# Four graph layers on 64 graphs: every issue time of a written-out plan replaced

## The chip, the cores and the metric

The kernel runs on one core of a Trainium2 chip, in one launch. The metric is the device time of that launch in microseconds (us). Several runs of the kernel before are given with their median; one more execution was profiled.

## The reference, cut to what matters

There are 64 independent graphs of 256 nodes with 512 features each, and a 256 x 256 adjacency matrix per graph. Each graph passes through four layers. Every layer begins with a layer norm over the features and a ReLU, and adds its result to `x`. All data are float32.

```python
# layer 0
h = relu(layernorm(x)); q, k = split(h @ W_qk); v = h @ W_v
x = x + softmax(sum((q @ k.T) / 8 * adj, -1), over nodes) * v
# layer 1: 8 heads of 64
h = relu(layernorm(x)); f = h @ W[head]
att = softmax(leaky_relu(e_self[:, None] + e_neigh[None, :]) + NEG_BIG * (1 - adj))
x = x + relu(att @ f + b)
# layer 2: 8 heads
h = relu(layernorm(x)); Xp = h @ Wp + bp; Xc = Xp @ C.T
x = x + relu(tanh(adj * (Xc @ Xp.T)) @ Xp)
# layer 3
h = relu(layernorm(x)); q, k = split(h @ W_qk); v = h @ W_v
x = x + softmax(q . (adj @ (k * mask)) / sqrt(512), over nodes) * v
```

## The kernel before, in words

**Steps and the plan.** The work of one graph is cut into 178 named steps. A step issues one to eight instructions on one engine, or DMAs on the queue of SyncE (SP). A table gives each step an issue time: `TIMES` holds the times for a graph in the steady state, relative to the start of its period; `FIRST` has tables of their own for the first nine graphs, `LAST` for the last eight, and `WEIGHTS` for the loading and preparing of the weights. A step of graph `b` gets the time `b * PERIOD + TIMES[step]`. `Plan.sequence` (line 619) sorts all steps of all graphs by that time, and `Plan.run` (line 627) issues them in this order and ties each instruction to the one before it on the same engine, so that no compiler moves them:

```python
steps += [(b * PERIOD + at, b, name) for name, at in times.items()]
return sorted(steps)
```

The times are not waited for on the chip. They only fix the order in which the instructions stand in each engine's queue. On the chip an engine takes its queue in order, and each instruction waits on semaphores for its own inputs and buffers. So five or six graphs are under way at once, interleaved step by step. Buffers (`big`, `bank`, `xt` and so on) are taken from lists when a step is issued and put back when their last user has been issued.

**The steps that matter here.** A name ends in the layer or in a part number.

- Layer 0: `load` (six DMAs), `st0 rs0 pw0 sh0 hn0` (norm), `sq0` (two 32 x 32 block transposes on VectorE, line 912), `sw0` (one DMA that writes the 512 KB tile to DRAM, line 1029), `ht0` (four DMAs that gather it transposed, line 917). Then `vsa`, `vsb` on GpSimd (lines 1065 to 1073) make sums, from which seven products `v1` to `v7` on TensorE (line 1081, two-by-two block products in seven multiplications) give `v` and the scores; `v1`, `v2`, `v4` need only what `ht0` brought, `v5`, `v6`, `v7`, `v3` need `vsa` or `vsb` too. VectorE adds them up (`vu vq vl0 vw vl1 vr0 vr1`, line 1095), `score0` (TensorE, line 1197), `s0v`, `softp0` (TensorE, line 1037), `softv0 softa0 softw0`, `add0`.
- Layer 1: `ms1 sx1 rs1 pw1 sh1 hn1 sq1 sw1 ht1` as above; `fa0`, `fa1` (TensorE, line 906, 272 columns wide), `fae0`, `fae1`, `send` (VectorE, lines 1246 to 1265), `er` (four small DMAs to DRAM), `enes` (two DMAs of 1 MB that bring the rows back to all partitions, lines 1275 and 1276); `max0` to `max3` (VectorE, line 1288, sixteen instructions), `mxv mxt mr mb`; per pair of heads `ea` (ScalarE), `eg` (GpSimd, line 1334), `eb` (VectorE, line 1340), `ex` (ScalarE), `po` (TensorE, line 1358), `eh` (GpSimd, line 1367); `sqo0`, `sqo1`, `swo` and `or` send the result through DRAM (lines 1163, 1029, 1179).
- Layer 2: `xp0 xp1` (line 906, 512 wide), `xe`, `sqx swx xpt`, `xc`, `ps0 ps1`, `tv`, `ta`, `py0 py1`, `sqy0 sqy1 swy yr`.
- Layer 3: `agg0 agg1` (line 1550), `sq3 sw3 ht3`, seven products `g1` to `g7` as in layer 0, `zs`, `softp3`, `add3`, `store`.

Every sheet that has to be transposed thus goes to DRAM and back (`sw` then `ht`), seven times for a graph, all on SP's queue.

Of the kernel before, what the change touches and what calls it, by code (L numbers as in the profile page):

```python
# [37 lines left out]
PERIOD = 53.0  # L38
TIMES = {
    "load": -55.958, "st0": -49.583, "rs0": -44.646, "pw0": -36.318, "sh0": -34.389, "hn0": -28.054, "sq0": -23.880,  # L40
    "sw0": -20.361, "at": -13.629, "ht0": -13.295, "vsa": -7.391, "vsb": -5.585, "v5": -5.238, "v6": -4.473,
    "v1": -4.435, "v2": -4.429, "va": -3.714, "v7": -3.586, "vu": -3.459, "v4": -0.672, "v3": -0.428, "vq": 0.560,
    "vw": 0.888, "vl0": 1.080, "vl1": 1.174, "score0": 1.287, "s0v": 2.823, "vr0": 3.678, "softp0": 6.233,
    "softv0": 7.190, "softa0": 8.025, "vr1": 8.143, "softw0": 11.863, "add0": 11.883, "ms1": 12.017, "sx1": 12.176,
    "rs1": 12.570, "pw1": 15.448, "sh1": 15.468, "hn1": 17.606, "sq1": 17.626, "sw1": 20.639, "ht1": 21.979,
    "fa0": 22.725, "fa1": 23.304, "fae0": 26.098, "fae1": 27.361, "send": 27.471, "er": 31.505, "enes": 34.142,
    "neg": 38.100, "max0": 40.266, "max2": 40.311, "ea1": 46.119, "max3": 47.873, "max1": 47.890, "negt": 49.291,
    "ea2": 51.375, "ea3": 55.720, "eg1": 57.348, "ea0": 61.604, "mxv": 61.732, "mxt": 61.752, "fb0": 64.897,
    "fbe0": 64.917, "mr": 70.776, "mb": 70.796, "eg3": 75.379, "eg2": 75.479, "fb1": 75.603, "eg0": 75.679,
    "fbe1": 77.982, "eb0": 78.082, "ex0": 78.102, "eb3": 78.275, "eb1": 78.325, "ex1": 78.337, "eb2": 78.397,  # L50
    "eh1": 79.204, "ex3": 79.228, "po0": 80.231, "po1": 80.682, "ex2": 80.783, "po2": 84.620, "po3": 85.301,
    "sqo0": 85.445, "eh0": 88.783, "su0": 88.910, "sqo1": 91.326, "eh3": 91.549, "swo": 91.587, "eh2": 94.253,
    "su1": 94.458, "se": 94.478, "or": 94.836, "sp": 95.038, "sr": 98.701, "om0": 101.429, "om1": 101.861,
    "oa0": 101.861, "oa1": 101.881, "sx2": 102.438, "rs2": 103.930, "pw2": 103.950, "sh2": 104.354, "hn2": 104.374,
    "sq2": 107.686, "sw2": 109.636, "ht2": 119.000, "xp0": 125.880, "xe0": 126.367, "xp1": 127.317, "xe1": 128.965,
    "sqx": 129.657, "swx": 130.649, "xpt": 135.864, "xc": 138.845, "xcv": 146.041, "xca": 146.061, "ps1": 146.081,
    "tv2": 146.101, "tv3": 146.151, "ta2": 149.074, "ps0": 149.878, "tv1": 150.250, "ta3": 150.686, "py1": 151.759,
    "tv0": 151.889, "ta1": 152.589, "ta0": 152.972, "py0": 154.569, "sqy0": 155.545, "sqy1": 158.087, "swy": 160.787,
    "yr": 168.125, "yp0": 169.206, "yp1": 169.226, "ya1": 171.370, "ya0": 171.420, "sx3": 174.829, "rs3": 174.849,
    "am": 177.436, "pw3": 178.663, "sh3": 179.490, "hn3": 179.510, "sq3": 179.709, "sw3": 180.291, "agg1": 181.480,  # L60
    "agg0": 181.703, "ht3": 186.025, "gsa": 195.020, "ga0": 195.034, "g4": 196.820, "ga1": 197.203, "zd": 198.118,
    "gsb": 200.495, "g2": 200.888, "g5": 202.877, "g6": 213.565, "g1": 219.162, "xa": 221.007, "g3": 224.216,
    "uu": 224.644, "g7": 225.065, "uq": 227.417, "uw": 227.437, "zc": 227.478, "uc1": 230.511, "za": 233.117,
    "zb": 234.865, "zs": 235.303, "softp3": 235.361, "softv3": 242.009, "uc0": 243.772, "softa3": 248.324,
    "softw3": 248.344, "add3": 248.611, "store": 256.387,
# [3 lines left out]
    "wn0": -2754.166, "mt0": -2695.235, "mv0": -2547.881, "mm0": -2545.730, "wa": -1191.640, "wqk": -1154.337,  # L69
    "wn1": -1149.788, "wv0": -1139.027, "mt1": -1138.916, "mv1": -1138.119, "t0": -1137.526, "w10": -1127.290,  # L70
    "sa0": -1126.945, "b1": -1092.446, "wn2": -988.967, "mm1": -985.862, "wn3": -953.396, "w11": -932.270,
    "sa1": -887.977, "mt2": -885.804, "w12": -880.346, "w13": -874.980, "mv2": -504.503, "mt3": -499.542,
    "mm2": -499.507, "sa3": -487.647, "sa2": -487.190, "mv3": -407.047, "w21": -337.874, "wv3": -333.465,
    "mm3": -316.473, "mk": -300.627, "mkp": -208.048, "ma": -204.797, "w22": -179.666, "mkv": -174.873,
    "w20": -173.107, "w23": -159.368, "b2": -147.136, "c2": -38.328, "mt": -12.051, "room": 111.231,
# [1534 lines left out]
```

## Time and profile before

| what | value |
|---|---|
| runs of the kernel | 3685.83 us median of 3 (3681.97 to 3687.0) |
| the profiled execution, its own time | 3695.39 us |
| its span, first to last instruction | 3693.3 us |
| TensorE granted clock | 0.985 of full speed |
| TensorE, VectorE, ScalarE, GpSimd busy | 3494.9, 3251.5, 2415.6, 1623.2 us |
| DMA moved | 785.00 MB, mean 213 GB/s |
| store of graph 9 issued, of graph 52 issued | 783.9 us, 3145.8 us: 43 rounds of 54.93 us |

What lies around the span is 2.1 us. Between the ninth and the fifty-third graph the kernel is in a steady round of 54.93 us, one graph coming out of each; the rest is the filling at the start and the draining at the end. A busy TensorE counts pipelined matrix products from their start to a modelled end, so that its share says little of how much room is left; the distances of their starts say more.

### The profile page before, as it was taken

What the parts mean: (1) busy time and instruction counts of PE and PEld (TensorE: products, weight loads), DVE (VectorE), ACT (ScalarE), POOL (GpSimd) and SP (SyncE); (2) the same over time, 40 slices, a digit from 0 to 9 for tenths busy, and PEclk for the clock granted to TensorE, in tenths of its full rate; (3) what the DMA queues carried; (4) which work ended last, traced back from release to release, by engine and by line L of the source; (5) the groups of instructions that cost most, each with busy time, mean ns of one, the idle gap of its engine ahead of it and who ended that gap; (6) DMA issues with size and microseconds to landing.
All of it is one profiled execution on the core that took longest, in us unless ns stands there. A gap on an engine that the chain in (4) does not pass through costs nothing.

```text
span 3693.3 us, 57357 instructions
## 1 busy us (share of the span) xinstructions
PE 3494.9 (95%) x16322; PEld 2031.4 (55%) x16322; DVE 3251.5 (88%) x8558; ACT 2415.6 (65%) x5381; POOL 1623.2 (44%) x1811
## 2 busy tenths in 40 slices
PE   6889999999999999999999999999999999998988
PEld 3555555555555555555555555555555555555544
DVE  6789898999898999999999899899899999898866
ACT  2567666667667667667766767667666766656654
POOL 2454444454444454444454444354444444343441
PEclk8899999999999999999999999999999999999999
DMA  6667666776776777777777777777677777676643
GB/s 192 196 217 218 211 213 199 223 222 217 222 220 211 224 223 221 227 228 217 222 229 211 223 224 212 219 234 214 216 231 219 221 224 221 198 215 190 210 149 120
DMA packets 967467, 785.00 MB, mean 213 GB/s; under 512 B 788912, under 2 KB 859120, under 8 KB 942576
## 3 DMA queue, kind: packets, MB, share of 16 engines
q1 hardware_dynamic: 967152, 781.34, 69.0%
q8 instruction: 132, 2.16, 0.2%
q14 instruction: 183, 1.50, 0.1%
HBM read 511.12 MB, written 270.01 MB: 211 GB/s over the span
## 4 chain that ended last, share of the span: by engine, by line
DVE 32%; PE 24%; DMA 19%; ACT 10%; issue 7%; SPq 6%; POOL 2%; DVEq 0%; ACTq 0%; POOLq 0%
DMA big<-sq_d 9%; DMA sq_d<-big 9%; PE bank L1081 8%; PE bank L906 7%; DVE big L912 6%; DVE big L1095 5%; ACT big L1416 5%; DVE big L1340 4%; PE bank L1358 3%; SPq L917 2%; SPq L1179 2%; DVE big L1163 2%; ACT big L974 2%; DVE bank L1135 2%; PE bank L1487 2%
## 5 line engine op out<-in xcount | busy, mean ns | idle before, releaser
L906 PE MATMUL bank<-w_s,big 128*128 128x256 f32 (+2 forms) x3072 | 956.1, 462 | 48.7 <-DMA big<-sq_d 42.6
L906 PEld LDWEIGHTS bank<-w_s,big 128*128 128x128 f32 x3072 | 604.3, 199 | 435.1 <-issue 281.9
L1081 PE MATMUL bank<-t_s,big 128*128 128x320 f32 (+1 forms) x1536 | 610.1, 528 | 39.2 <-POOL big L1065 31.2
L996 POOL TENSOR_TENSOR rstd<-rstd,power 128x2 f32<-128x2 f32 x256 | 178.9, 699 | 1053.6 <-DVE rstd L990 999.2
L1334 POOL TENSOR_TENSOR big<-big,negt 128x1024 f32<-128x1024 f32 x256 | 605.8, 2389 | 21.6 <-ACT big L1327 18.0
L1288 DVE CUSTOM_DVE_ANT_0 junk<-all,adj 128x256 f32<-128x256 f32 x1024 | 485.9, 475 | 32.2 <-DMA all<-er_d 1.5
L1346 ACT ACTIVATE big<-big 128x1024 f32<-128x1024 f32 x256 | 258.8, 1051 | 389.6 <-DVE big L1340 388.6
L1367 POOL TENSOR_TENSOR half<-big 128x512 f32<-128x512 f32 x256 | 325.2, 1291 | 424.9 <-ACT big L1346 288.9
L1009 ACT ACTIVATE big<-xt,shift,rstd 128x512 f32<-128x512 f32 x512 | 383.4, 805 | 171.4 <-POOL shift L1002 169.2
L912 DVE STREAM_TRANSPOSE big<-big 128x512 f32<-128x512 f32 x640 | 472.6, 774 | 19.4 <-ACT big L1009 18.9
L1327 ACT ACTIVATE big<-all,ec 128x256 f32<-128x256 f32 x1024 | 428.1, 494 | 80.2 <-DMA all<-er_d 76.4
L1095 DVE TENSOR_TENSOR big<-bank,big 128x320 f32<-128x320 f32 (+1 forms) x704 | 393.9, 568 | 35.4 <-PE bank L1081 19.9
L1081 PEld LDWEIGHTS bank<-t_s,big 128*128 128x128 f32 x1536 | 280.6, 194 | 241.9 <-issue 121.3
L1511 DVE TENSOR_TENSOR big<-bank,at 128x512 f32<-128x512 f32 x512 | 318.1, 673 | 48.1 <-PE bank L1487 46.7
L1518 ACT ACTIVATE big<-big 128x512 f32<-128x512 f32 x512 | 294.1, 625 | 85.5 <-DVE big L1511 81.2
L1081 PE MATMUL bank<-w_s,big 128*128 128x320 f32 x1024 | 323.0, 448 | 11.6 <-ACT big L1103 3.8
L1065 POOL TENSOR_TENSOR big<-big 128x256 f32<-128x256 f32 x128 | 110.3, 862 | 502.9 <-DMA big<-sq_d 462.3
L1340 DVE TENSOR_TENSOR big<-big,all 128x1024 f32<-128x1024 f32 x256 | 304.0, 1245 | 1.9 <-DMA all<-m_d 1.5
L974 ACT ACTIVATE big<-xt,sum 128x512 f32<-128x512 f32 x384 | 272.7, 711 | 42.0 <-DVE sum L1226 29.1
L1416 ACT ACTIVATE big<-big,rs 128x64 f32<-128x64 f32 x1024 | 251.5, 333 | 64.0 <-DMA big<-sq_d 51.8
L1487 PE MATMUL bank<-big,big 64*128 64x256 f32 x2048 | 260.0, 392 | 4.8 <-DVE bank L1135 4.3
L1358 PE MATMUL bank<-big,big 128*64 128x256 f32 x2048 | 243.1, 386 | 17.2 <-ACT big L1346 16.7
(119 smaller groups left out, 5300.0 us busy)
## 6 DMA issues: line engine op xcount, KB each, us to landing
sq_d<-big SPq DMA_DIRECT2D x448, 512.0 KB
big<-sq_d SPq DMA_DIRECT2D x1792, 128.0 KB
all<-er_d SPq DMA_DIRECT2D x128, 1024.0 KB
all<-m_d SPq DMA_DIRECT2D x64, 1024.0 KB
xt<-in_x_dram SPq DMA_DIRECT2D x64, 512.0 KB
out_dram<-xt SPq DMA_DIRECT2D x64, 512.0 KB
adj<-in_adj_dram SPq DMA_DIRECT2D x64, 256.0 KB
blocks<-in_adj_dram SPq DMA_DIRECT2D x256, 64.0 KB
```

The source lines that it names most:

```text
L906: nc.tensor.matmul(p, chunk(ht[:, k], c), w[:, k], start=(k == 0), stop=(k == KC - 1))
L912: nc.vector.transpose(sq.rearrange("p (r k i c) -> p c k r i", r=4, k=KC, c=NC)[:, c], t[:, c])
L974: nc.scalar.activation(g["hn"][:, c, :], g["xt"][:, c, :], AF.Square, scale=-float(D), bias=st["sum"][:, c:c + 1], accum_out=st["ssq"][:, ...
L1009: nc.scalar.activation(g["hn"][:, c, :], g["xt"][:, c, :], AF.Relu, bias=st["shift"][:, c:c + 1], scale=st["rstd"][:, c:c + 1])
L1081: nc.tensor.matmul(p, a()[:, k], w[:, k], start=(k == 0), stop=(k == 1))
L1095: nc.vector.tensor_tensor(out(), g[i][:, :w], old(), OP.add)
L1288: nc.vector.tensor_tensor_reduce(junk, g["en"][:, h, :], g["adj"][:, c, :], 1.0, -BIG, OP.add, OP.max, g["mx"][:, c, h:h + 1])
L1327: nc.scalar.activation(e[:, s, j, :], g["es"][:, h, :], AF.Prelu, bias=st["ec"][:, j, H + h:H + h + 1], alpha=0.2)
L1334: nc.gpsimd.tensor_tensor(e, e, g["negt"][:, None].to_broadcast([P, 2, NC, N]), OP.add)
L1340: nc.vector.tensor_tensor(e, e, g["m"][:, 2 * p:2 * p + 2, None, :].to_broadcast([P, 2, NC, N]), OP.subtract)
L1358: nc.tensor.matmul(po[s * U:(s + 1) * U, p % 2, :], feats[:, j, h * U:(h + 1) * U], e[:, s, j, :], start=(j == 0), stop=(j == NC - 1))
L1416: nc.scalar.activation(normal_rows(2)[:, c, h * U:(h + 1) * U].rearrange("p (a i) -> p a i", a=2), y[:, h // 2, h % 2 * 2:h % 2 * 2 + 2], ...
```

## The change

Only the tables `PERIOD`, `TIMES`, `WEIGHTS`, `FIRST` and `LAST` change. No step, no instruction, no tile and no buffer count is altered; the order of the queues is. `FIRST` and `LAST` keep their nine and eight tables, with every time new. The lines of the diff that hold the steps named here:

```diff
-PERIOD = 53.0
+PERIOD = 52.8
 TIMES = {
-    "load": -55.958, "st0": -49.583, "rs0": -44.646, "pw0": -36.318, "sh0": -34.389, "hn0": -28.054, "sq0": -23.880,
-    "sw0": -20.361, "at": -13.629, "ht0": -13.295, "vsa": -7.391, "vsb": -5.585, "v5": -5.238, "v6": -4.473,
-    "v1": -4.435, "v2": -4.429, "va": -3.714, "v7": -3.586, "vu": -3.459, "v4": -0.672, "v3": -0.428, "vq": 0.560,
-    "vw": 0.888, "vl0": 1.080, "vl1": 1.174, "score0": 1.287, "s0v": 2.823, "vr0": 3.678, "softp0": 6.233,
-    "fa0": 22.725, "fa1": 23.304, "fae0": 26.098, "fae1": 27.361, "send": 27.471, "er": 31.505, "enes": 34.142,
+    "load": -39.563, "st0": -11.544, "rs0": -7.386, "pw0": -7.277, "sh0": -7.257, "neg": -6.117, "hn0": -2.912,
+    "sq0": -0.951, "sw0": 1.023, "ht0": 8.345, "vsa": 9.031, "v2": 10.708, "at": 11.189, "v1": 12.329, "v5": 12.373,
+    "va": 12.902, "v6": 13.291, "vsb": 13.821, "vu": 14.671, "vl0": 14.721, "v7": 15.867, "v4": 15.981, "vq": 18.814,
+    "vw": 19.471, "vl1": 20.118, "score0": 20.138, "s0v": 20.835, "softp0": 21.256, "v3": 22.258, "softv0": 25.597,
+    "ht1": 46.450, "fa0": 48.029, "fa1": 49.125, "fae0": 50.298, "fae1": 50.987, "send": 51.284, "er": 52.645,
+    "enes": 54.413, "max0": 61.658, "max2": 64.992, "max1": 65.589, "ea2": 66.135, "fb1": 70.598, "max3": 73.438,
...
 WEIGHTS = {
-    "wn0": -2754.166, "mt0": -2695.235, "mv0": -2547.881, "mm0": -2545.730, "wa": -1191.640, "wqk": -1154.337,
+    "wn0": -3088.720, "mt0": -3061.312, "wa": -2989.984, "mv0": -2986.374, "wn1": -2972.348, "w10": -2970.224,
...
```

Sorted, the steady tables give these queues for one round. The number in brackets is the graph relative to the one whose `score0` begins the list.

```
TensorE before: score0[0] g6[-4] softp0[0] g1[-4] fb0[-1] g3[-4] g7[-4] xp0[-2] xp1[-2] agg1[-3] fb1[-1] agg0[-3]
  fa0[0] fa1[0] softp3[-4] po0 po1 po2 po3[-1] xc[-2] su0[-1] g4[-3] ps1[-2] su1[-1] g2[-3] sp[-1] g5[-3] ps0[-2]
  py1[-2] v5[1] v6[1] v1[1] py0[-2] v2[1] v7[1] v4[1] v3[1] | score0[1] g6[-3] softp0[1] ...
TensorE after:  score0[0] g4[-4] softp0[0] v3[0] fb0[-1] g5[-4] g2[-4] xp0[-2] xp1[-2] agg0[-3] g7[-4] po2[-1]
  fa0[0] fa1[0] agg1[-3] g1[-3] softp3[-4] xc[-2] su0 po0 po1 po3 su1[-1] ps0[-2] ps1[-2] g6[-3] g3[-3]
  v2[1] sp[-1] v1[1] v5[1] v6[1] py0[-2] py1[-2] v7[1] v4[1] fb1[0] | score0[1] g4[-3] softp0[1] ...
SP, both:       swy[-3] sw2[-2] yr[-3] ht2[-2] mr[-1] mb[-1] sw1[0] sw3[-3] ht1[0] swx[-2] ht3[-3] xpt[-2] er[0]
  sw0[1] enes[0] swo[-1] ht0[1] or[-1] store[-4] load[2]
VectorE before, around fae: sqx[-2] fbe1[-1] eb0 eb3 eb1 eb2[-1] fae0[0] fae1[0] send[0] sq0[1] softv3[-4] uc0[-4]
  sqo0[-1] softw3 add3[-4] sqo1[-1] zd[-3] at[1] tv2 tv3[-2] max0[0] max2[0] tv1[-2] sr[-1] tv0[-2] max3[0] max1[0]
VectorE after, around fae:  sqx[-2] eb0 eb1[-1] uc0 zd[-4] fae0[0] uw zc[-4] fae1[0] send[0] eb3[-1] zs[-4] sq0[1] uc1[-4]
  softv3 za[-4] sqo0 sqo1[-1] softw3 add3[-4] tv1[-2] max0[0] tv0 tv3 tv2[-2] at[1] sr[-1] max2[0] max1[0]
GpSimd before, around vsa:  eh1 eh0[-1] gsa[-3] eh3 eh2[-1] gsb[-3] vsa[1] vsb[1] pw2 sh2[-1] eg1[0]
GpSimd after, around vsa:   eh0 eg3[-1] gsa[-3] eh1 eh3 eh2[-1] gsb[-3] vsa[1] vsb[1] pw2 sh2[-1] eg2[0]
```

In `WEIGHTS` and the first table of `FIRST` the DMAs at the start change places as well. Before, `ht0` of graph 0 comes behind `load`, `wn0`, `wa`, `wqk`, `wn1`, `sw0` and `wv0`. After, it comes behind `wn0`, `wa`, `load`, `wn1`, `w10`, `wn2`, `wqk`, `wn3`, `w13`, `sw0` and `wv0`.

## The prediction

> **What bounds the kernel now.** I read the page first, then the steady rounds, then one round step by step. Page, span and engines:
>
> ```profile
> span 3693.3 us, 57357 instructions
> PE 3494.9 (95%) x16322; PEld 2031.4 (55%) x16322; DVE 3251.5 (88%) x8558; ACT 2415.6 (65%) x5381; POOL 1623.2 (44%) x1811
> ```
>
> TensorE looks full, but its busy time is modelled. The Trainium skill says the same of matmul busy time (Perfetto Trace Analysis, "Identifying the Most-Contended Engine"), and the trace agrees: 512-column products of line 1081 last 606 ns by the groups of instructions, yet four of them begin at 1295.07 us in the timeline and the next step at 1296.85, 0.44 us each. Adding such start distances over all steps of a round gives about 53 us of TensorE work, an estimate from the timeline (the widths are below); the round is 54.93. So some 2 us a round are waits, and something other than TensorE's work closes the round.
>
> One round, in stretches (columns: width, then busy PE, PEld, DVE, ACT, POOL, granted clock, DMA share, GB/s):
>
> ```profile
> 1242.00:1262.00 20.00, 19.81 (x57) 10.44 (x56) 19.03 (x52) 13.53 (x30) 10.75 (x12) 1.00 0.70 220
> 1262.00:1266.00 4.00, 4.00 (x20) 3.24 (x21) 4.00 (x7) 2.57 (x3) 0.38 (x1) 1.00 0.98 233
> 1266.00:1270.00 4.00, 4.00 (x44) 2.48 (x48) 3.86 (x12) 3.75 (x8) 3.70 (x4) 1.00 0.61 161
> 1270.00:1282.00 12.00, 12.00 (x80) 6.36 (x74) 9.59 (x27) 5.91 (x12) 3.76 (x4) 1.00 0.92 289
> 1282.00:1297.00 15.00, 14.23 (x70) 8.86 (x67) 14.00 (x42) 12.49 (x34) 6.64 (x8) 1.00 0.58 194
> ```
>
> In the fourth stretch the 16 DMA engines are 92% busy at 289 GB/s. SP's queue there (start, duration, line; `er`, `sw0`, the two of `enes`, `swo`, `ht0`):
>
> ```profile
> 1266.63 1.90 SPq L1271 DMA_DIRECT2D er_d<-er  x4
> 1268.62 0.37 SPq L1029 DMA_DIRECT2D sq_d<-big  x1
> 1269.72 0.34 SPq L1275 DMA_DIRECT2D all<-er_d  x1
> 1270.11 0.45 SPq L1276 DMA_DIRECT2D all<-er_d  x1
> 1271.94 0.32 SPq L1029 DMA_DIRECT2D sq_d<-big  x1
> 1272.37 5.25 SPq L917 DMA_DIRECT2D big<-sq_d  x4
> ```
>
> Who waits for the last of them, in GpSimd's timeline (`vsa`; idle before it in brackets):
>
> ```profile
> 1282.82 0.85 POOL L1065 TENSOR_TENSOR big<-big 128x256 f32<-128x256 f32 x1 [7.76 <-DMA big<-sq_d]
> ```
>
> And TensorE's timeline: `softp0`, `fa0` with `fa1`, `v5` with `v6`, and the next graph's `softp0`:
>
> ```profile
> 1242.34 0.38 PE L1037 MATMUL bank<-ident,wc 128*128 128x128 f32 x2
> 1261.83 3.91 PE L906 MATMUL bank<-w_s,big 128*128 128x272 f32 x16 [0.19 <-DMA big<-sq_d]
> 1283.73 2.42 PE L1081 MATMUL bank<-t_s,big 128*128 128x320 f32 x8 [0.47 <-POOL big L1065]
> 1296.85 0.38 PE L1037 MATMUL bank<-ident,wc 128*128 128x128 f32 x2
> ```
>
> The reader sees a closed loop, from `softp0` of one graph to `softp0` of the next:
>
> - `softp0` end 1242.7 to `fa0` 1261.8: 19.1 us (softmax, norm, `sw1`, `ht1`);
> - `fa0` to the end of `fa1` 1265.7: 3.9;
> - to the landing of `ht0` 1282.8: 17.1;
> - `vsa` before `v5`: 0.9;
> - `v5` 1283.7 to the end of `softp0` 1297.2: 13.5.
>
> That is 54.5. `ht0` of the next graph does not use `enes` of this one; it only stands behind it. From `sw0` to `ht0`, 0.5 + 2 + 0.5 + 0.5 = 3.5 MB are queued, in 14.2 us. I call this loop the bound. The page agrees: "DMA big<-sq_d" and "DMA sq_d<-big" are 9% each of its chain, "L1081 <-POOL" and "L906 <-DMA" TensorE's largest waits (31.2 and 42.6 us in the groups of lines).
>
> **What the skill says.** "DMA: Bandwidth & Descriptors", "Queues, rings and completion order": descriptors on one engine are consumed in ring order. The trace agrees: `ht0` is issued by 1277.6 and lands at 1282.8. "SBUF — State Buffer", "SBUF: two separate sides": VectorE with two SBUF inputs and GpSimd lock a port pair for a whole instruction. The trace agrees (minimum, median, maximum in ns; a GpSimd `eg` takes 2389):
>
> ```profile
> L1288 DVE CUSTOM_DVE_ANT_0 junk<-all,adj x1024: 362/424/2447, 70.1 to 3570.5; 128x256 f32<-128x256 f32 x171
> ```
>
> Its mean on the page is 475, so the lock costs these about 1024 x 51 ns = 52 us of VectorE in all, 0.8 us a round.
>
> **The change, part by part.** It removes and adds no instruction. SP's queue keeps its order in the steady round, so no DMA is moved past another there. What moves is TensorE's, VectorE's, ScalarE's and GpSimd's work inside the loop. Step widths, from start distances in the timeline of this round: `v` 1.1 us, `g`, `agg`, `fb` 1.75, `xp` 3.45, `po` 0.9, `ps`, `py` 1.92, `xc` 1.0, `su` 0.6, `sp`, `softp` 0.3, `score0` 0.95.
>
> 1. `softp0` to `fa0`. TensorE work between them before: `g1 fb0 g3 g7 xp0 xp1 agg1 fb1 agg0`, 7 x 1.75 + 6.9 = 19.1 us, so that `fa0` hardly waits (0.19). After: `v3 fb0 g5 g2 xp0 xp1 agg0 g7 po2`, 1.1 + 5 x 1.75 + 6.9 + 0.9 = 17.7. The way through softmax, norm and DRAM keeps its steps. `mr` and `mb` move ahead a little with an earlier `sq2`, so I take 18.9 for 19.1. TensorE now waits 1.2 at `fa0`. On the path: -0.2.
> 2. `fa0`, `fa1`: unchanged, 3.9.
> 3. `fa1` to the landing of `ht0`. On VectorE `uw` and `zc` (0.69 + 0.76) come between `fae0` and `fae1`, but `fa1` takes 1.95 after `fa0`, which hides them if VectorE isn't late. `eb3` (1.24) and `zs` (0.53) come between `send` and `sq0`. Before, `sw0` waited for SP to finish `er` (1268.5), not for `sq0` (1267.8); now `sq0` ends 1.8 later, 1269.6, and `enes` behind it 0.4 later. `swo` follows `po3`, which moves from 3.8 to 7.9 us after `fa1` (`agg1 g1 softp3 xc su0 po0 po1 po3`). Its issue goes to about +8.9 instead of +6.2. `enes` keeps the DMA engines busy to about +13, so this costs nothing; without that cover it would cost 2.7. Sum 17.5: +0.4.
> 4. `vsa`. `v2`, `sp` and `v1` now stand before `v5`. They need only `ht0`, and `vsa` (0.85) hides behind their 2.5 us. The 0.9 becomes 0.1: -0.8.
> 5. First product to `softp0`. Before, `v5 v6 v1 py0 v2 v7 v4 v3 score0 g6 softp0`: 7 x 1.1 + 1.92 + 0.95 + 1.75 + 0.3 = 12.6 of work and 0.9 of waits (0.30 of it at `score0`). After, `v2 sp v1 v5 v6 py0 py1 v7 v4 fb1 score0 g4 softp0`: 6 x 1.1 + 0.3 + 3.84 + 1.75 + 0.95 + 1.75 + 0.3 = 15.5 of work, with `score0`'s wait covered by `fb1`. `max3` (1.8) and `sq2` stand before `s0v` on VectorE, beside `g4`'s 1.75; I put nothing for it. +2.0.
>
> Sum of the loop: 18.9 + 3.9 + 17.5 + 0.1 + 15.5 = 55.9 against 54.5: +1.4. Not every round is tight: in some `v5` waits for TensorE alone, and part of the added work fills waits elsewhere. I take +0.9 a round, with -0.5 to +1.9 as its bounds: the low one if the waits of step 3 shorten by 2 us, the high one if `eb3`, `max3` or a lock falls on the path. Over 52 rounds, from the 47 graphs of `TIMES` and their neighbours: +47 us.
>
> **The lock.** In the new order `max2` and `max1` still follow `sr`, beside `gsb`, `vsa` and `vsb` on GpSimd, and three of the transposes (`sq1`, `sq3`, `sq0`) still lie by `eg`. I count no gain; at most the 52 us of VectorE go, which is not the loop.
>
> **Start and end.** At the start 1.5 MB more (`wn2`, `wn3`, `w10`, `w13`) go ahead of `ht0` of graph 0. At the 200 GB/s of the first slices that is 7.5 us later for the first products; `mm1` to `mm3` then fill it. TensorE is idle 59 us of the first 200. I take +3, from -15 to +20. The tail is ordered anew, and the trace doesn't show that order: 31 us of TensorE are idle after 3500. I take 0, from -15 to +15.
>
> **Sum.** +50 us, on the profiled execution 3695.4 to 3745. The median of the runs shown is 9.6 lower, so 3685.8 to **3736 us**.
>
> **Rivals.**
>
> - *The wait at `v5` goes and nothing takes its place* (faster). The trace has TensorE waiting 31 us for GpSimd at line 1081, 43 for DMA at line 906 and 20 for VectorE at line 1197, 94 us in all. TensorE now has `agg1 g1 softp3 xc su0 po0 po1 po3 su1 ps0 ps1 g6 g3`, 16.0 us, between `fa1` and `v2`. If `ht0` lands within that, and VectorE loses its 0.8 us a round of locks, some 39 us go: 3647. For it: `vsa` is hidden. Against: landing took 17.1, and those MB don't shrink. It decides where the landing falls under 16 us.
> - *SP and DMA alone set the round* (no change). SP's order is the same, so is the loop of transfers; TensorE's added work in step 5 fits beside it. 3686. Against: `swo`'s place is shifted easily by TensorE. That the change does nothing because times are only an order belongs here.
> - *VectorE becomes the bound* (slower still). It is gap-free for most of 1249 to 1272. If `eb3`, `max3` and `sr`'s later `sp` all push `vl1` and `s0v`, +1.9 a round: 3785.
>
> **How the numbers follow.** The loop longer: 0.55, with its own range 3700 to 3775. VectorE the bound: 0.10. Faster: 0.25. No change: 0.10. A measurement of this kernel can tell about 0.2% (7 us) from nothing, so faster by over 0.2% is 0.25, within 0.10, slower 0.65. Leaving out about a tenth at either side, the range is 3645 to 3790.
>
> **What would show it.** In the profile after: rounds of 55.8 us; TensorE waiting for "DMA big<-sq_d" at line 1081 (`v2`) in place of GpSimd, and more at line 906 (`fa0`); 17 to 18 us from `fa1`'s end to `ht0`; 15.5 or more from `v2` to `softp0`. Wrong if `v2` starts without a wait, or rounds stay below 54.7.

## The result, and the profile after

The changed kernel takes 3844.56 us, the median of 4 runs (3837.82 to 3849.44), against 3686.41 us of the kernel before on the same chip (3681.97 to 3687.59). The ratio is 1.043, interval 1.041 to 1.045: slower by 158 us. The forecast said slower, 3736 us, with a range up to 3790. Its direction was right and its size was not.

The profiled execution of the changed kernel took 3847.72 us, its span is 3845.9. The lines of after carry numbers that are 3 lower than those of before (L903 for L906, L1078 for L1081, and so on). First the page of after, span and engines:

```profile
span 3845.9 us, 57782 instructions
...
PE 3528.7 (92%) x16322; PEld 2066.3 (54%) x16322; DVE 3332.4 (87%) x8558; ACT 2432.0 (63%) x5381; POOL 1667.3 (43%) x1811
```

Nothing was added, and yet TensorE, VectorE, ScalarE and GpSimd are all busy longer, while their shares of the span fall. That is what waits look like on a page: all engines lose share together. Where the loss lies is told by the times at which the stores are issued:

| store of graph | 0 | 9 | 52 | 63 | span |
|---|---|---|---|---|---|
| before | 269.3 | 783.9 | 3145.8 | 3689.5 | 3693.3 |
| after | 281.0 | 811.2 | 3297.5 | 3842.2 | 3845.9 |

Up to the store of graph 9, 27.3 us are lost. The 43 rounds to graph 52 lose 124.4 (57.82 us a round instead of 54.93, so 2.89 each), and the end loses 0.9. One steady round in stretches, in windows of after that answer to those of before (columns: width, then busy PE, PEld, DVE, ACT, POOL, granted clock, DMA share, GB/s). `fa1` ends at 1079.2, `v2` starts at 1098.3:

```profile
1075.30:1079.20 3.90, 3.90 (x19) 3.37 (x18) 3.87 (x9) 2.12 (x2) 2.65 (x2) 1.00 1.00 257
1079.20:1082.20 3.00, 3.00 (x9) 1.23 (x7) 3.00 (x6) 0.00 (x0) 2.92 (x3) 1.00 0.74 167
1082.20:1085.20 3.00, 2.51 (x30) 0.96 (x30) 3.00 (x7) 1.53 (x2) 2.12 (x2) 1.00 0.03 6
1085.20:1095.20 10.00, 10.00 (x71) 6.26 (x72) 8.43 (x22) 5.39 (x12) 3.78 (x4) 1.00 1.03 338
1095.20:1098.30 3.10, 0.61 (x2) 0.00 (x1) 2.68 (x5) 2.62 (x5) 0.00 (x0) 1.00 0.63 142
1098.30:1102.30 4.00, 3.97 (x10) 2.66 (x11) 1.44 (x8) 1.31 (x7) 2.84 (x4) 0.57 0.67 231
```

Three things are to be seen. From 3 to 6 us after `fa1` the DMA engines are 3% busy, and then 103% for ten. From 1095.2 on, TensorE works 0.61 of 3.1 us. And in the four microseconds after that its clock is 0.57. Who was late is in SP's queue of the same round (start, duration, line; `er`, `sw0`, the two of `enes`, `swo`, `ht0`):

```profile
1081.32 1.71 SPq L1268 DMA_DIRECT2D er_d<-er  x4
1084.35 0.34 SPq L1026 DMA_DIRECT2D sq_d<-big  x1
1084.91 0.34 SPq L1272 DMA_DIRECT2D all<-er_d  x1
1085.30 0.63 SPq L1273 DMA_DIRECT2D all<-er_d  x1
1088.77 0.32 SPq L1026 DMA_DIRECT2D sq_d<-big  x1
1089.14 4.47 SPq L914 DMA_DIRECT2D big<-sq_d  x4
```

`sw0` goes out 5.1 us after the end of `fa1` (before: 2.9), and `enes` stands behind it. `sw0` waits for `sq0`, so VectorE's timeline from `uw` to `sq0` comes next:

```profile
1078.12 0.69 DVE L1092 TENSOR_TENSOR big<-bank,big 128x512 f32<-128x512 f32 x1
1078.85 1.85 DVE L1132 SCALAR_TENSOR_TENSOR bank<-big,mask_s,big 128x512 f32<-128x512 f32 x1
...
1080.63 0.18 DVE L1243 COPY ec<-bank 128x32 f32<-128x32 f32 x1
...
1081.06 0.23 DVE L1262 STREAM_TRANSPOSE er<-ec 128x64 f32<-128x64 f32 x1
1081.22 1.26 DVE L1337 TENSOR_TENSOR big<-big,all 128x1024 f32<-128x1024 f32 x1
1082.40 0.69 DVE L1151 TENSOR_TENSOR wc<-wc 128x2 f32<-128x2 f32 x1
1083.02 0.70 DVE L909 STREAM_TRANSPOSE big<-big 128x512 f32<-128x512 f32 x1
```

In this order these are `uw`, `zc`, `fae1`'s first half, `send`, `eb3`, `zs`, `sq0`. `fa1` was done at 1079.2, but `fae1` starts at 1080.6 behind a `zc` of 1.85 us, and two more steps stand between `send` and `sq0`. GpSimd's timeline says why `zc` is so long (`eg3`, then `gsa`, and at last `vsa`, with its idle time in brackets):

```profile
1077.80 2.34 POOL L1331 TENSOR_TENSOR big<-big,negt 128x1024 f32<-128x1024 f32 x1
1080.11 1.29 POOL L1062 TENSOR_TENSOR big<-big 128x256 f32<-128x256 f32 x1
1081.48 1.60 POOL L1063 TENSOR_TENSOR big<-big,big 128x256 f32<-128x256 f32 x1
...
1098.35 0.84 POOL L1062 TENSOR_TENSOR big<-big 128x256 f32<-128x256 f32 x1 [9.26 <-DMA big<-sq_d]
```

`eg3` runs until 1080.14, and by the page cited in the prediction it holds the port pair as long; `zc` ends half a microsecond after it. Over all 64 graphs `zc` went from a median of 0.76 us to 1.85 (the line of `zc`: minimum, median, maximum in ns; before, then after):

```profile
L1135 DVE SCALAR_TENSOR_TENSOR bank<-big,mask_s,big x64: 707/760/2904, 258.0 to 3683.4; 128x512 f32<-128x512 f32 x64
```

```profile
L1132 DVE SCALAR_TENSOR_TENSOR bank<-big,mask_s,big x64: 752/1845/2817, 260.9 to 3836.3; 128x512 f32<-128x512 f32 x64
```

TensorE's timeline gives the end of the wait, `v2` and `v1` (four matmuls each; `v7`, of the same form, takes 1.34 us later in this round), and the `softp0` that closes the round. The `softp0` before it was at 1057.41:

```profile
1098.33 2.01 PE L1078 MATMUL bank<-w_s,big 128*128 128x320 f32 x4 [2.52 <-DVE at L935]
...
1100.55 2.08 PE L1078 MATMUL bank<-w_s,big 128*128 128x320 f32 x4
...
1114.96 0.38 PE L1034 MATMUL bank<-ident,wc 128*128 128x128 f32 x2
```

Over the whole run, the groups of lines (busy, mean ns, idle before) say the same. In the kernel before, the group with `v5`, which came first there, and the group of `v1`, `v2`, `v3` and `v7`:

```profile
L1081 PE MATMUL bank<-t_s,big 128*128 128x320 f32 (+1 forms) x1536 | 610.1, 528 | 39.2 <-POOL big L1065 31.2 <-DVE big L1095 5.1 <-ACT big L1103 2.1
L1081 PE MATMUL bank<-w_s,big 128*128 128x320 f32 x1024 | 323.0, 448 | 11.6 <-ACT big L1103 3.8 <-DMA big<-sq_d 3.4 <-DVE big L1095 2.5
```

The second of them after:

```profile
L1078 PE MATMUL bank<-w_s,big 128*128 128x320 f32 x1024 | 380.1, 502 | 125.4 <-DMA big<-sq_d 78.1 <-DVE at L935 44.8 <-DVE big L1508 1.7
```

"DVE at L935" is named for a part of the wait, but `at` isn't what `v2` waits for: in the first experiment below `v2` starts 2.1 us before `at` ends. The two came at about the same time here. `v2` starts a median of 0.2 us before `vsa`, which waits for the same landing.

### The profile page after: what moved, and what is told of

The parts are those of the page before. It is cut to its first block, busy times and chain, and to the rows that moved or that the text cites. A ratio compares the mean times of both kernels' runs of the same rounds, so it can differ in the third digit from the quotient of the medians.

```text
span 3845.9 us, 57782 instructions
## 1 busy us (share of the span) xinstructions
PE 3528.7 (92%) x16322; PEld 2066.3 (54%) x16322; DVE 3332.4 (87%) x8558; ACT 2432.0 (63%) x5381; POOL 1667.3 (43%) x1811
## 5 line engine op out<-in xcount | busy, mean ns | idle before, releaser
L903 PE MATMUL bank<-w_s,big 128*128 128x256 f32 (+2 forms) x3072 | 955.2, 462 | 42.1 <-DMA big<-sq_d 38.2
L903 PEld LDWEIGHTS bank<-w_s,big 128*128 128x128 f32 x3072 | 604.8, 199 | 382.6 <-issue 281.0
L1078 PE MATMUL bank<-t_s,big 128*128 128x320 f32 (+1 forms) x1536 | 603.9, 523 | 4.7 <-DVE big L1160 2.4
L909 DVE STREAM_TRANSPOSE big<-big 128x512 f32<-128x512 f32 x640 | 483.2, 783 | 19.4 <-ACT big L1006 16.6
L1078 PE MATMUL bank<-w_s,big 128*128 128x320 f32 x1024 | 380.1, 502 | 125.4 <-DMA big<-sq_d 78.1
L1343 ACT ACTIVATE big<-big 128x1024 f32<-128x1024 f32 x256 | 268.8, 1054 | 351.2 <-DVE big L1337 346.3
L1285 DVE CUSTOM_DVE_ANT_0 junk<-all,adj 128x256 f32<-128x256 f32 x1024 | 459.5, 449 | 30.8 <-DMA all<-er_d 2.0
L1515 ACT ACTIVATE big<-big 128x512 f32<-128x512 f32 x512 | 302.9, 628 | 211.9 <-DVE big L1508 211.4
L1062 POOL TENSOR_TENSOR big<-big 128x256 f32<-128x256 f32 x128 | 126.6, 989 | 627.0 <-DMA big<-sq_d 377.9
L1078 PEld LDWEIGHTS bank<-t_s,big 128*128 128x128 f32 x1536 | 292.4, 197 | 196.5 <-issue 114.3
L1337 DVE TENSOR_TENSOR big<-big,all 128x1024 f32<-128x1024 f32 x256 | 328.1, 1308 | 18.3 <-DMA all<-m_d 9.2
L1078 PEld LDWEIGHTS bank<-w_s,big 128*128 128x128 f32 x1024 | 205.6, 219 | 245.1 <-DVE at L935 81.6
L971 ACT ACTIVATE big<-xt,sum 128x512 f32<-128x512 f32 x384 | 273.0, 712 | 92.3 <-DVE sum L1223 60.9
L1355 PE MATMUL bank<-big,big 128*64 128x256 f32 x2048 | 257.9, 395 | 44.6 <-ACT big L1343 40.9
```

Of the source, the lines that this page charges most:

```text
L903: nc.tensor.matmul(p, chunk(ht[:, k], c), w[:, k], start=(k == 0), stop=(k == KC - 1))
L909: nc.vector.transpose(sq.rearrange("p (r k i c) -> p c k r i", r=4, k=KC, c=NC)[:, c], t[:, c])
L1078: nc.tensor.matmul(p, a()[:, k], w[:, k], start=(k == 0), stop=(k == 1))
L1285: nc.vector.tensor_tensor_reduce(junk, g["en"][:, h, :], g["adj"][:, c, :], 1.0, -BIG, OP.add, OP.max, g["mx"][:, c, h:h + 1])
L1337: nc.vector.tensor_tensor(e, e, g["m"][:, 2 * p:2 * p + 2, None, :].to_broadcast([P, 2, NC, N]), OP.subtract)
L1515: nc.scalar.activation(g[f"th{p}"][:, s], g[f"th{p}"][:, s], AF.Tanh)
```

## The experiments

Numbers given "a round" are means over graphs 10 to 51 of the profiled execution, each step's times read from the trace and counted from the end of `fa1`. Every time is the median of its runs; its ratio is to the kernel before on the same chip, where the changed kernel has 1.043. The kernel before took 3682 to 3688 us beside them, so times from two chips compare to some 5 us. An inserted line moves the line numbers by one against those of after or before.

My theory: the loop of the prediction is right, and VectorE's order between `fa1` and `sq0` lengthens it, since `sw0` holds everything behind it on SP's queue; the half clock after the wait adds to it. The rivals: VectorE's throughput, a buffer behind `swo`, TensorE's own work.

**One step of VectorE put back.** After, with

```diff
+TIMES.update({"sq0": -1.512})      # fae0 uw zc fae1 send sq0 eb3 zs
```

> The changed kernel with one time altered: sq0 stands directly behind send on VectorE, ahead of eb3 and zs. Theory A (the loop fa1, send, er, sw0, enes, ht0, v2, softp0 sets the round, and what VectorE puts between fa1 and sq0 lengthens it): sw0 and enes are issued some 1.3 us earlier, the wait at v2 (2.7 us a round now) shrinks by as much, and 47 rounds give -60 us: about 3785, rounds of 56.5. Rival B (VectorE's own throughput is the bound): the same instructions in another order, 3845 within 10. Rival C (v2 waits for a buffer that swo's landing frees, not for ht0): no change, 3845.

Measured: 3740.4 us, ratio 1.0136 (1.0109 to 1.0164); 104 us less, for one time out of 178. A round is 55.53. `sw0` goes out at +3.93 instead of +5.04, `enes` at +4.96 instead of +5.61, and `vsa`, which waits for the landing of `ht0`, starts at +17.44 instead of +19.41. `v2` waits 0.05 us instead of 2.49. It gave more than I expected for two reasons. The landing gained 2.0 and not 1.3, and `v2` to `softp0` fell from 16.79 to 15.53: the half clock went too. The first line below is the group of `v2` again, with 9.6 us of waits where it had 125.4. What came in its place is in the second, the group of `softp0` and `softp3`: `softp3` waits for `zs` (`wc` of line 1152), 1.92 us a round:

```profile
L1079 PE MATMUL bank<-w_s,big 128*128 128x320 f32 x1024 | 326.5, 444 | 9.6 <-DMA big<-sq_d 7.6 <-ACT big L1516 1.3 <-DVE big L1509 0.5
...
L1035 PE MATMUL bank<-ident,wc 128*128 128x128 f32 x256 | 60.7, 302 | 99.0 <-DVE wc L1152 92.2 <-DVE bank L1203 6.3
```

Rival B (throughput) and rival C (a buffer behind `swo`) fall: `swo` goes out 1.65 us later here than in the changed kernel, and the round is still shorter.

**The other step put back, and both.** After, with

```diff
+TIMES.update({"uw": 262.65, "zc": 262.67})                  # e2: fae0 fae1 send eb3 uw zc zs sq0
+TIMES.update({"sq0": -1.512, "uw": 262.65, "zc": 262.67})   # e3: fae0 fae1 send sq0 eb3 uw zc zs
```

> The changed kernel with two times altered: uw and zc stand behind send and eb3, so that fae1 and send follow fae0 directly. Theory A: send no longer stands behind zc (1.80 us now, 0.76 before, drawn out beside GpSimd's eg3); er is written about 1.1 us earlier, but sq0 comes no earlier, since eb3, uw, zc and zs still stand ahead of it. If er's way to enes decides, -1.1 us a round, about 3795; if sw0 decides (it stands ahead of enes on the queue of SP and waits for sq0), 0: 3845, or slightly slower. Rival B (VectorE's throughput): only the lock of zc goes, at most -1 us a round and the same whatever stands behind it.

Measured: 3868.41 us, 1.048 (1.045 to 1.0511), 24 us worse than the changed kernel. `send` ends at +0.77 instead of +1.91 and `er` goes out 0.8 earlier, as foreseen. But `sq0` ends at +6.31 instead of +5.01 and `enes` goes out at +6.91. So an early `er` brings nothing; `sw0` decides, and it is ahead of `enes`.

> The changed kernel with both edits: VectorE has fae0 fae1 send sq0 eb3 uw zc zs. Theory A: from the end of fa1 to the landing of ht0 17 to 17.3 us again instead of 19.2, v2's wait falls from 2.7 to under 1 us, and with it the half clock after it: -2 to -2.5 us a round, about 3740, near the forecast of 3736. Rival B (VectorE's throughput) at most -1 us a round: 3800. Rival C (buffer behind swo): no change.

Measured: 3791.92 us, 1.0283 (1.0261 to 1.0305). It failed by 52 us. `sw0` and `enes` are back at +3.22 and +4.26, where they were before, and `v2` waits 0.08 us. But `zs` now ends at +5.64 behind `eb3`, `uw` and `zc`, and the wait is at `softp3`, ahead of `v2` on TensorE:

```profile
L1035 PE MATMUL bank<-ident,wc 128*128 128x128 f32 x256 | 59.8, 302 | 127.8 <-DVE wc L1152 119.0 <-DVE bank L1203 6.1 <-DMA sq_d<-big 2.6
```

That is 2.57 us a round there. The work that follows, `po3` and `swo` with it (+12.2), is late by as much, and `ht0` behind `swo` lands at +18.35, not at the 17 to 17.3 expected. The wait had only moved.

**The half clock alone.** After, with the two matmuls of `g3` issued twice, ahead of `v2`:

```diff
-                    for k in range(2):
+                    for k in (0, 1, 0, 1) if name == "g" and i == 3 else (0, 1):
```

> The changed kernel, with the two matmuls of the product g3 issued twice (the second pair starts the sum anew; +1.7 us of TensorE work a graph, just ahead of v2 where TensorE idles). Theory A with the clock (the idle of 3 us before v2 makes TensorE run at half clock for the next 3 us): the added work lies in the wait, v2 starts at the same time, and the half clock behind it goes: -0.5 to -0.8 us a round, 3805 to 3822. If the half clock costs nothing on the path: 3845. Rival D (TensorE's own work is the bound): +1.7 us a round, 3925.

Measured: 3814.3 us, 1.0338 (1.0314 to 1.0362). TensorE got 1.7 us more work a graph and the kernel is 30 us faster. The landing did not move (`vsa` at +19.45), and `v2` starts at the same time (19.34 us after `fa1` instead of 19.27). But `v2` to `softp0` takes 15.82 us instead of 16.79, and the same group has its short matmuls again:

```profile
L1078 PE MATMUL bank<-w_s,big 128*128 128x320 f32 x1024 | 333.6, 451 | 52.4 <-DMA big<-sq_d 28.0 <-DVE at L935 20.6 <-DVE mx L1285 1.2
```

In windows of all steady rounds the granted clock is 0.97 in the changed kernel and 1.00 here. Rival D (TensorE's work is the bound) falls.

**The fault put into the kernel before.** Before, with

```diff
+TIMES.update({"sq0": -20.554})     # fae0 fae1 send softv3 uc0 sqo0 sq0
```

> The kernel before with one time altered: sq0 stands on VectorE behind softv3, uc0 and sqo0 instead of ahead of them (0.38 + 0.67 + 0.69 = 1.75 us, as much as eb3 and zs take in the changed kernel). It puts the one suspected fault into the kernel before, with all other orders as they were. Theory A (a late sq0 holds sw0, and sw0 holds enes and ht0 behind it on the queue of SP; v5 then waits, and TensorE goes to half clock): sq0 ends about 4.9 us after fa1 instead of 2.1, ht0 lands at 19.2 instead of 17.4, the round grows by 1.8 to 2.9 us: 3780 to 3835. Rival (sq0's place mattered only together with the changed kernel's own orders, for instance its earlier enes or later swo): at most +0.5 us a round, below 3715.

Measured: 3735.18 us, 1.015 (1.0126 to 1.0174), 53 us slower than the kernel before. That lies between the two: theory A had 3780 to 3835, the rival below 3715. It is less than theory A had, since the three steps did not wait and `sq0` ended at +4.11 instead of the assumed 4.9. `enes` came 0.5 later, the landing 0.8, and the wait at `v5` grew from 0.73 to 1.29 us a round. `POOL big` is `vsa` here, behind which the landing stands; before it had 39.2 us of waits:

```profile
L1082 PE MATMUL bank<-t_s,big 128*128 128x320 f32 (+1 forms) x1536 | 616.3, 532 | 72.2 <-POOL big L1066 61.3 <-DVE big L1096 4.1 <-ACT big L1104 3.5
```

The mechanism works in the other kernel too, but smaller: a third of the loss of the changed kernel, and in the traced execution, which took 3727 us, 0.59 us a round instead of 2.89. There 27 of the 37 waits stay under 2.2 us, and TensorE has 6 periods of half clock where the trace of before has 5. The rest of the loss belongs to `sq0`'s place together with the other orders of the changed kernel.

**Both waits taken away, and what is late next.** After, with

```diff
+TIMES.update({"sq0": -1.512, "zs": 262.56})     # e5: fae0 uw zc fae1 send sq0 zs eb3
+              "fb1": 63.5, "softp3": 264.315    # e10, besides: fb1 ahead of v2, softp3 behind xc or su0
+              "uw": 261.4855, "zc": 261.487     # e11, besides: uw zc ahead of fae0
```

> The changed kernel with two times altered: sq0 directly behind send as before it, and zs ahead of eb3 behind sq0, so that VectorE has fae0 uw zc fae1 send sq0 zs eb3. With sq0 alone moved, v2 waited 0.05 us a round, but softp3 waited 1.92 us for zs, and the round was 55.53. Theory A (once ht0 lands in time, TensorE's way to v2 decides, and that is its work of 16.0 us and softp3's wait): the wait at softp3 falls to some 0.5 us, v2 reaches the landing again and waits up to 1 us there; a round of 54.2 to 54.8, 3665 to 3700. Rival B (VectorE's throughput is by now the bound): no change from the 3740 of sq0 alone.

Measured: 3712.0 us, 1.0073 (1.0054 to 1.0091). A round is 55.02, with 0.62 us of waits at `v2` and 0.72 at `softp3`. So two times in the table take back 133 of the 158 us, and the steady round is within 0.1 us of the one before. Rival B said no change, and falls again; my range was missed by 12 us.

> The changed kernel with sq0 and zs directly behind send, and besides fb1 ahead of v2 and softp3 behind su0 on TensorE (fb1's 1.75 us fill the wait at v2, and softp3 waits for zs no longer). With sq0 and zs alone the round was 55.02 with waits of 0.62 at v2 and 0.72 at softp3. If TensorE's work and these waits make the round: 55.02 - 1.3 + 0.3 (score0's wait, which fb1 covered) = 54.0, 47 rounds of -1.0: 3665. If VectorE, 89% busy, has become the bound: 3712 within 10.

Measured: 3746.94 us, 1.0183 (1.0168 to 1.0198). It failed, and so did its rival: 35 us slower than without the edit. The waits at `v2` and `softp3` are gone as meant (0.12 and none). In their place TensorE waits for VectorE inside `score0` and at `softp0`; `fb1` had covered both. From `score0`'s start to the next step it is now 1.67 us instead of 0.91 (`low` is what `vl1` writes, line 1203 `s0v`'s):

```profile
L1035 PE MATMUL bank<-ident,wc 128*128 128x128 f32 x256 | 66.1, 307 | 31.3 <-DVE bank L1203 26.1 <-DVE wc L1152 5.0
L1195 PE MATMUL bank<-low,at 128*128 128x64 f32 x256 | 53.7, 291 | 30.3 <-DVE low L1093 30.3
```

The edit was made in full only in part of the rounds. The new time of `softp3` falls together with that of `su0`, and the rounding of the sums puts it behind `su0` in 11 of the 42 rounds and ahead of it, right behind `xc`, in the others. From one end of `fa1` to the next, the 11 take 55.11 us and the others 55.76; the waits inside `score0` and at `softp0` are 0.5 and 0.4 us in both. So the edit as it was meant gains nothing on the 55.02 either, and what makes the loss of 35 us isn't told apart. e11 and e12 have the same rounds.

> As e10_fb1_softp3, with uw and zc ahead of fae0 on VectorE, so that zc is no longer between fae0 and fae1. It asks what the port lock costs on the way: zc takes 1.80 us there beside GpSimd's eg3 and 0.76 alone. If zc is out of eg3's way, send comes 1.0 us earlier and enes 0.6; since v2 no longer waits, the time stays within 10 us of e10. If zc still meets a GpSimd instruction, fae0 is late instead and the gain is nil or a loss of up to 0.5 us a round.

Measured: 3753.46 us, 1.0201 (1.0173 to 1.0229), the same as e10. `zc` met `eg3` there too: it now runs from -1.21 to +1.01, 2.2 us long, and `fae0` comes at +1.70 instead of -1.01. The lock went with the step. What it costs on the way isn't told apart: no run here has `zc` in its place without the lock.

**Step 4 alone, and `swo` out of the way of `ht0`.** Before, with the first, the second and both lines; after, with the third, besides `sq0` and `zs` as in e5:

```diff
+TIMES.update({"v2": -5.26, "v1": -5.25})    # e6, e14: v2 v1 v5 v6
+TIMES.update({"ht0": -14.5})                # e13, e14: er sw0 enes ht0 swo
+TIMES.update({"ht0": 4.4})                  # e15: er sw0 enes ht0 swo
```

> The kernel before with two times altered: v2 and v1 stand ahead of v5 on TensorE, as in the changed kernel. This is step 4 of the prediction alone. By its price vsa (0.9 us) hides behind v2 and v1: up to -0.8 us a round over 52 rounds, -40: 3646. By the waits that the trace of before shows in the steady rounds (v5 waits 0.73 us a round on average, some of it for ht0 itself, which v2 needs too) some -0.5 a round: 3660. If the bound is VectorE or the ring of transfers: 3686 within 7.

Measured: 3683.51 us, 0.9995 (0.9986 to 1.0004): nothing that can be told. `vsa` is hidden, and the wait of 0.73 at `v5` becomes 0.11 at `v2`, but `score0`'s grows from 0.17 to 0.39 and 0.10 appears at `v7`.

> The kernel before with one time altered: ht0 stands ahead of swo on the queue of SP (er sw0 enes ht0 swo), so that 0.5 MB less is queued ahead of it. Theory A (what is queued ahead of ht0 sets its landing): it lands about 1.7 us earlier (0.5 MB at the 289 GB/s of that stretch), v5's wait of 0.73 us a round goes, TensorE's own work and VectorE are then the bound: -0.3 to -0.7 a round, 3650 to 3670. Rival (swo and or, now later, are what comes late next: or lands some 3 us later, and oa and sx2 behind it): no gain or up to +1 us a round, 3686 to 3740.

Measured: 3713.08 us, 1.0069 (1.0051 to 1.0087). The landing comes even 2.7 us earlier (`vsa` at +14.62), so what is queued ahead of `ht0` does set it. The kernel is slower nonetheless, as the rival had it. `or` lands later behind `swo`, and `oa0` and `oa1` (line 961, in the experiment 962) wait on VectorE ahead of `vu` and `vl1`. The group in the kernel before, then in e13:

```profile
L961 DVE SCALAR_TENSOR_TENSOR xt<-big,xt 128x512 f32<-128x512 f32 x256 | 176.3, 714 | 68.8 <-ACT big L1416 38.4 <-ACT big L1529 28.6 <-issue 0.4
```

```profile
L962 DVE SCALAR_TENSOR_TENSOR xt<-big,xt 128x512 f32<-128x512 f32 x256 | 177.8, 714 | 126.0 <-ACT big L1417 96.4 <-ACT big L1530 29.2
```

(ScalarE, named there, is the step between `or` and `oa`.) `v5` waits no more, but `v7` waits 0.55, by the trace for `va` on ScalarE, and `score0` 0.62 for VectorE.

> As e13_b_ht0_swo, with v2 and v1 ahead of v5 on TensorE as in e6_v2v1_first. Under theory A landing and vsa are then both hidden, and only score0's wait for VectorE is left: a round of 54.2 to 54.5, 3650 to 3665. Under the rival the same as e13.

Measured: 3709.26 us, 1.0061 (1.0045 to 1.0077), as e13 and as the rival said.

> The changed kernel with sq0 and zs directly behind send (3712) and ht0 ahead of swo on the queue of SP. v2 waited 0.62 us a round there. Theory A: ht0 lands 1.5 us earlier and this wait goes; softp3's wait of 0.72 stays: a round of 54.4, 3685. Rival: swo and or late, no gain, 3712 or more.

Measured: 3749.55 us, 1.0164 (1.014 to 1.0188), 38 us slower than e5. The landing is 1.9 us earlier and `v2` waits no more; `oa1` waits 1.15 us a round, `v7` 0.55, `softp0` 0.40.

**The start.** After, with the transfers of the start as before (e7); these and on VectorE `rs1` and `sq1` of graph 0 ahead of most weight sums, on e10 (e12); these and the norm of graph 1 up to `sq0` ahead of them too, on e5 (e16):

```diff
+WEIGHTS.update({"wqk": -2973.0, "w10": -2597.0, "wn2": -2596.0, "wn3": -2595.0, "w13": -2594.0, ...
+FIRST[0].update({n: FIRST[0][n] - 200 for n in ("load", "st0", "rs0", "pw0", "sh0", "hn0", "sq0")})
+FIRST[0].update({"sx1": -705.5, "rs1": -705.0, "pw1": -704.9, "sh1": -704.8, "hn1": -704.7, "sq1": -633.5})  # e12, e16
+FIRST[1].update({"load": -690.0 - PERIOD, "st0": -641.0 - PERIOD, ..., "sq0": -633.4 - PERIOD})              # e16
```

> The changed kernel with the start put near that of before: load of graph 0 stands first on the queue of SP, wqk ahead of wn1, and w10, wn2, wn3, w13 behind ht0 of graph 0, w23 and w21 behind load of graph 2; the steps that need these weights (mt2 mv2 mm2 mt3 mv3 mm3 sa0 sa1 sa3) follow softp0 of graph 0. The steady tables and the other tables of the start are those of the changed kernel. The changed kernel issued the store of graph 0 11.7 us later than before and that of graph 9 27.3 us later. If the order of the first transfers is the cause of the whole, -20 to -27 us: about 3820. If it is only the first step of it, -8 (the delay of softp0 of graph 0), and the rest comes from the tables of the first nine graphs: 3836. If the pipeline fills the gap, as the forecast had it: no change, 3845.

> As e10_fb1_softp3, with the start of before: the transfers as in e7_start, and on VectorE rs1 and sq1 of graph 0 ahead of most of the weight sums (sa0 to sa3). In e7_start softp0 of graph 0 came 10 us earlier, but the weight sums then stood ahead of rs1 and fa0 of graph 0 came 3 us later. If that was why nothing was gained, fa0 of graph 0 comes at 50 to 56 us (61.6 in the changed kernel, 52.5 before) and the time is 8 us below e10. If the later tables of the start make the loss, as much as e10 within 5 us.

> The changed kernel with sq0 and zs directly behind send (3712), and the start of e12_fb1_start with the norm of graph 1 as well (load st0 rs0 pw0 sh0 hn0 sq0) ahead of the weight sums sa0, sa3, sa2, as in the kernel before. If the order at the very start makes the loss, fa0 of graph 0 comes at 50 to 56 us instead of 61.9, the store of graph 0 at 270, and 8 to 12 us of the time go: 3702. If the tables of graphs 1 to 8 make it, fa0 of graph 0 comes early and the gain is gone again at graph 9: 3712 within 5.

| us | before | after | e7 | e12 | e16 |
|---|---|---|---|---|---|
| `softp0` of graph 0 | 34.1 | 42.1 | 31.9 | 31.4 | 31.8 |
| `fa0` of graph 0 | 52.5 | 61.6 | 64.6 | 65.8 | 57.5 |
| store of graph 0 | 269.3 | 281.0 | 284.5 | 286.2 | 273.0 |
| store of graph 9 | 783.9 | 811.2 | 818.1 | 811.1 | 795.5 |
| median of the runs | 3686.4 | 3844.6 | 3841.3 | 3751.0 | 3702.3 |

The first products came 10 us earlier in all three. In e7 that was worth nothing (1.0429, 1.0401 to 1.0457), nor in e12 (1.0192, 1.017 to 1.0213, where e10 has 1.0183). One run more, e8, puts e7's start on e5 and was expected to gain 8 to 25 us: 3710.53 us, 1.0065 (1.0042 to 1.0089), the same as e5. The weight sums, 14 us of VectorE, then stood ahead of `rs1`; with that mended in e12, `sq0` of graph 1 still stood behind them (it ends at 60.2 us), and `sw0` of graph 1 stands ahead of `ht1` of graph 0 on SP's queue. Only with the norm of graph 1 up to `sq0` moved as well (46.3 us) does `fa0` come early, and the time falls by 10 us against e5: 1.0036 (1.0022 to 1.005). It is the same fault as in the steady round: a late transpose holds a store, and the store holds a foreign gather. The other 12 us up to graph 9 stay open; what is left there is the order of graphs 0 to 8 among themselves.

None of these kernels beats the kernel before. e6 stands level with it, e16 is 0.36% behind.

## Why the direction was right and the size wrong

That the loop of the prediction sets the round is shown by e1, e2 and e4. Its steps follow one another, so they add up to a round whatever the cause, and each can be held against its figure. The first column is the one round that the prediction read; "mean" is over graphs 10 to 51:

| step | before, one round | before, mean | forecast | after, mean |
|---|---|---|---|---|
| 1. `softp0` to `fa0` | 19.1 | 19.21 | 18.9 | 17.67 |
| 2. `fa0`, `fa1` | 3.9 | 3.95 | 3.9 | 3.99 |
| 3. and 4. `fa1` to the first product | 18.0 | 18.36 | 17.6 | 19.27 |
| 5. first product to `softp0` | 13.5 | 13.42 | 15.5 | 16.79 |
| sum | 54.5 | 54.94 | 55.9 | 57.72 |

The direction was in part luck. The forecast got its +1.4 from step 5, with step 1 held at 18.9. With the 17.7 that step 1 took, its own sum is 54.7 against 54.5, hardly a change. e5 shows the same: step 5 takes 15.75 us there, step 1 17.68, and the round is 55.02. What made the steady rounds longer is the step that the forecast put at +0.4 and the half clock that it did not have.

- **Step 1, wrong by -1.2.** I took the way through softmax, norm and DRAM to be 18.9 us and TensorE's work 17.7, so that `fa0` would wait 1.2. TensorE's work was right, and `fa0` waits 0.11; line 903 waits 38.2 us for DMA in all, where I had expected more than the 42.6 of before. The way itself got shorter than I had let it: counted from the end of `softp0`, `sq1` starts at 8.15 us instead of 9.84, `sw1` goes out at 9.60 instead of 11.17 and `ht1` at 12.49 instead of 14.16. I had given the new order 0.2 us of this way, and it took at least 1.5. Which of the moved steps did it no run separates.
- **Step 3, wrong by +1.9.** This is the step that failed. I hid `uw` and `zc` behind `fa1` "if VectorE isn't late", with the 0.76 us that `zc` takes alone. It took 1.85, and `fae1` started 1.4 us after `fa1`. I let `sq0` end 1.8 later, and it was 2.9. And I let `enes` come only 0.4 later: it came 1.3 later, and `sw0` ahead of it 1.8 (+5.04 instead of +3.24). The landing was 2.05 later (+19.41 instead of +17.36). It followed `sw0`, which it comes 14.1 us behind before and 14.4 after, more than `enes` (13.0 and 13.8). The prediction had named this as its upper bound, +1.9 "if `eb3`, `max3` or a lock falls on the path": `eb3` did, and the lock. The cover named for `swo`'s later issue held in e1, where `swo` goes out at +11.2 and the landing is at +17.4, as before; in e3, with `swo` at +12.2, it didn't.
- **The lock, sign by place.** "I count no gain" was near the truth for `max`, which got back half of its 52 us. What I had not counted is the 1.1 us that `zc` got longer between `fae0` and `fae1`, ahead of `send`. e2 has `send` 1.1 us earlier without it; how much of the 2.89 is due to it alone no run shows.
- **Step 4, right, and worth nothing.** `vsa` is hidden in the changed kernel. That it would have been worth 0.8 in the kernel before was an error: e6 gives 3 us in all, within the noise. Another wait, `score0`'s for VectorE, stood just behind it.
- **Step 5, the work right, the clock forgotten.** Where TensorE's clock holds in this stretch, in e1 and e3, `v2` to `softp0` takes 15.53 us: the sum of distances was right to a tenth. In the changed kernel it is 16.79. Between 800 and 3150 us its trace has 32 periods of half clock with 122.9 us together (before: 5 with 17.1). Half of that over 41 rounds is 1.5 us a round, and 1.0 us is what e4 gave back in this stretch.
- **The discount.** I took 0.9 of the 1.4, since "not every round is tight". It was the wrong way: a wait that is there in nearly every round leaves none loose.
- **The start.** Its first step was right (7.5 us for the transfers; `softp0` of graph 0 came 8.0 later). "`mm1` to `mm3` then fill it" was not: +27.3 stood at graph 9 where I had +3.

`max`'s group in the changed kernel, where the mean was 475 ns before:

```profile
L1285 DVE CUSTOM_DVE_ANT_0 junk<-all,adj 128x256 f32<-128x256 f32 x1024 | 459.5, 449 | 30.8 <-DMA all<-er_d 2.0
```

In the terms of the sum: 43 rounds of 2.89 are 124.4, where 0.9 gives 38.7. That is 86 of the 103 us by which the span missed (152.6 against 50), and the rest is mostly the start. e1 and e4 tell how the 2.89 divide. Putting `sq0` back, and nothing else, takes 2.29 of it. About 1 us of these is the half clock that the wait brings with it. Of the other 0.6, putting `zs` ahead of `eb3` takes 0.5 (e5), and 0.1 is left.

The rivals: "slower, VectorE as the bound" came nearest by its number, 3785, but not by its cause. e1 has VectorE's instructions in another order and gains 104 us. "SP and DMA alone" had a true part, since SP's order is what hands the delay of `sq0` to `enes`. The order on SP stayed the same; when its head became ready did not. The faster rival asked for a landing under 16 us, and it was 19.4.

## What to carry to other kernels

Where a queue is taken in order, price a moved step by what stands behind its consumer there: here 1.75 us of VectorE ahead of one transpose held a store, and the store held 3 MB of other transfers behind it while the DMA engines were 3% busy for 3 us. When a sum leaves a wait of some microseconds on TensorE in each round, add the slower clock after it, here about 1 us; work put into the wait, even useless work, gave 30 us back. And before a wait is counted as a gain, look for the second wait right behind it: seven of these runs (e1, e3, e6, e10, e13, e14, e15) took TensorE's wait away at one place and found one of 0.4 to 2.6 us at another.

## What the runs showed of the hardware that was not expected

**The clock after a wait.** In 38 steady rounds of the changed kernel, `v2` waited under 2.2 us in 8 and no half clock followed; it waited longer in 30, and in 29 of them TensorE's clock fell to half. The periods last 3.41 us, four of them 6.83. The Trainium skill ("TensorE: Matmul & The Clock Gate", Part 1) has the clock halved after an idle window of about 3.4 us and full again after as long a busy one. The length of the slow period agrees. The wait that suffices was shorter here, and no fixed one: single waits of 1.87 us (before) and 1.95 us (e4) were followed by a half clock, while in e9 five of the ten waits from 2.3 us on, up to 3.0, were not.

**The lock lengthens both sides.** Beside VectorE's `eb3`, the second instruction of `gsa` on GpSimd takes 1.60 us in the round shown, against 0.73 for the same line in `vsa`; in e10, where `eb3` comes 2 us later, it takes 0.74 (median). And `zc`, with both big inputs in SBUF, ends 0.56 us after the `eg3` that it met, the median of the changed kernel, of e10 and of e11 alike: moving it ahead of `fae0` (e11) changed its start but not its end. The page has the later of the two fully blocked until the other is done. Here `zc` still needed 0.56 us after that, not the 0.76 that it takes alone.
